# Graph attention and neighbour quantiles on one core: five record blocks in one sequence with scatters between gathers, and compare networks over two tiles at once in a planned order

## The chip, the cores and the metric

The kernel runs on one core of a Trainium2 chip. The metric is the device time of that core in microseconds (us), the median of the runs shown. One execution was taken by the hardware profiler. The engines are called PE (matrix multiply), PEld (its weight loads), DVE (vector), ACT (scalar), POOL (GpSimd, which here issues almost nothing but indirect DMAs) and SP (which issues plain DMAs).

## What is computed

There are 4,096 nodes with 128 features and an adjacency matrix of 0 and 1 in which a row holds 11 to 55 ones, 32 on average. The first layer is graph attention with 8 heads, the second replaces each node by quantiles of its neighbours:

```python
Wh = einsum('nd,hde->hne', nodes, W)
e  = leaky_relu(f1[:, :, None] + f2[:, None, :])      # f1 = Wh.a1, f2 = Wh.a2
h  = elu(softmax(where(adj > 0, e, -9e15)) @ Wh)      # 8 heads
x1 = layernorm(nodes + elu(concat(h) @ W1 + b1))
# second layer: drop every skip-th neighbour, sort the kept ones per feature
picked_q = sort(x1[kept neighbours], axis=0)[ceil(q * n_keep) - 1]   # q = .25 .5 .75
out = (0.5 * mean_q(picked_q) + 0.5 * x1) @ Wl.T + bl + x1
```

## The kernel before

Rows are worked in tiles of 128 nodes, one node to a partition, 32 tiles in all.

**First stage (attention).** `neighbours` reads the adjacency and leaves, on DVE, the list of up to 64 neighbours of each row of a tile (the search). `complete_records` finishes the records of a block of tiles, `rank_by_count` orders the block's rows by their number of neighbours, and indirect DMAs from POOL (`scatter`, L195) put the records into DRAM in that order. So the rows of one sorted tile have about equally many neighbours, and a tile needs few empty slots. There are three blocks, `BLOCKS = [4, 12, 16]` tiles, and a table `CAPS` says how many neighbours each sorted tile must hold. `layers` cuts that capacity into layers of 32, 16, 8 and 4 columns.

For one sorted tile, `list_rows` loads the records (`R`) and the narrow layers' lists with SP DMAs and transposes them on DVE. `fetch_rows` gathers neighbours from DRAM, one indirect DMA of 128 rows for each column of a layer (`gather`, L186, into the tile `G` or `Gs`). `G` has two buffers. `weigh_rows` makes the scores on DVE and ACT and multiplies on PE (`y`, L888). `transform` works on two or four finished tiles and leaves `x1` in the list `store`, from which POOL scatters it to DRAM. `step` puts this in order: the gathers of a tile, then the `x1` scatters, then the weighing of the tile before with pieces of the search between (`quota`). The order on every engine is the order in which the program is written (`manual_schedule`). At the end of a block all record scatters of the next block stand together on POOL. In the last block the records of all rows are scattered to `all_d` in the order of all 4,096 rows, for the second stage.

**Second stage (quantiles).** For each of 32 tiles POOL gathers `2 * HT[t]` neighbours' `x1` rows (22 to 62) into `vals`, of which there are five buffers and one for the largest tile (`most`). `quantile_out` runs a compare network over these slots on all 128 features at once. A stage of the network is cut into pieces of at most `TURN = 12` slots. The lower operand of a piece is first copied by ACT into a PSUM tile `low` (L1162), because DVE overwrites it; then DVE writes the minimum and the maximum (L1166). Pieces of fewer than four slots with one result are not copied. The pool `low_ps` has two buffers, and every piece takes a tile of its own:

```python
kept = lp.tile([P, TURN * D], F32, name="low")[:, 0 : k * m * D]
nc.scalar.copy(kept, low)
for end in ends:
    nc.vector.tensor_tensor(high if end else low, kept, high, ALU.max if end else ALU.min)
```

Two tiles run at a time, one stage of each in turn, the second begun when the first has eight stages left. At the end of a tile ACT scales the 3 to 14 slots that can hold a quantile (`u`, L1175), PE sums and multiplies them, and POOL scatters the result to the output.

A path for rows that exceed a capacity stands behind a flag at the end.

Of the kernel before, what the change touches and what calls it, by code (L numbers as in the profile page):

```python
# [24 lines left out]
P = 128  # L25
N = 4096
D = 128
# [19 lines left out]
CAPS = {  # L47
    4: [29, 33, 37, 63],
    12: [25, 27, 29, 30, 31, 32, 34, 35, 36, 38, 41, 63],
    16: [24, 26, 28, 29, 30, 31, 32, 32, 33, 34, 35, 36, 38, 39, 42, 63],  # L50
    32: [
        23, 24, 25, 26, 27, 27, 28, 29, 29, 30, 30, 30, 31, 31, 32, 32,
        33, 33, 34, 34, 35, 35, 36, 36, 37, 37, 38, 39, 40, 41, 44, 63,
    ],
}
BLOCKS = [4, 12, 16]

CAP = CAPS[NT]
# [4 lines left out]
HT = [(c - 1) // 2 for c in CAP]  # L63
LMAX = 2 * max(HT)
LMOST = 2 * sorted(HT)[-2]
TURN = 12
# [9 lines left out]
def layers(c):  # L76


    out = []
    s = 0  # L80
    for w in (32, 32, 16, 8, 4):
        if (c + 3) // 4 * 4 - s >= w:
            out.append((s, w))
            s += w
    return out
# [51 lines left out]
def pieces_of(g):  # L137


    b, k, stride, n = g  # L140
    if k == 1:
        parts = -(-n // TURN)
        out = []
        for i in range(parts):
            m = (n - sum(p[3] for p in out)) // (parts - i)
            out.append((b, 1, m, m))
            b += m
        return out
    if n >= TURN:
        return [p for i in range(k) for p in pieces_of((b + i * stride, 1, n, n))]  # L150
    parts = -(-k // (TURN // n))
    out = []
    for i in range(parts):
        kk = (k - sum(p[1] for p in out)) // (parts - i)
        out.append((b, kk, stride, n))
        b += kk * stride
    return out


def slots_of(tile_, g):  # L160

    b, k, stride, n = g
    if k == 1:
        return tile_[:, b : b + n, :].rearrange("p s d -> p (s d)")
    v = tile_[:, b : b + (k - 1) * stride + n, :]
    flat = v.rearrange("p s d -> p (s d)")

    return bass.AP(
        tensor=flat.tensor,
        offset=flat.offset,  # L170
        ap=[list(flat.ap[0]), [stride * D, k], [1, n * D]],
    )


def quantile_slots(t):


    ht = HT[t]
    slots = {ht - 1}
    for h in range((LOW[t] + 1) // 2 - 1, ht + 1):  # L180
        slots |= {ht - h + (h + 1) // 2 - 1, ht - h + (3 * h + 1) // 2 - 1}
    return slots

# [26 lines left out]
def kernel(  # L210
# [19 lines left out]
    recs_d = [dram.tile([n * P, REC], F32, name=f"rec{n}_d") for n in BLOCKS]  # L230
# [50 lines left out]
    for i in range(2):  # L281
        sets = {}
        for w, r in ROWS_OF.items():
            lists = const.tile([P, 32], I32, name=f"list{w}_{i}")
# [9 lines left out]
    for i, values in enumerate((LOW, CAP, HT)):  # L294
        for t, v in enumerate(values):
            if t == 0 or v != values[t - 1]:
                nc.gpsimd.memset(limits[:, i, t:], float(v))

# [18 lines left out]
    def search(t0, n):  # L317
        return neighbours(
            tc, adjp, rec, num, adj, range(t0, t0 + n), back, chunk
        )  # L320

    for _ in search(0, BLOCKS[0]):
        pass
# [15 lines left out]
    turn = [0]  # L339

    pools, uses = [attp], {}

    def step(fetch=None, pieces=None, quota=0, size=2, more=None):
        if fetch:
            weigh.append(fetch_rows(tc, pools, fetch, xt_d, uses))
        while store:
            scatter(nc, x1_d, *store.pop(0))
        if len(weigh) > 1 or (weigh and not fetch):
            R, parts = weigh.pop(0)
            place = len(members)  # L350
            members.append(R)
            turns = len(parts) + 9
            each = -(-quota // turns)
            done = 0
            for _ in weigh_rows(tc, attp, pools, pp, parts, turned, place, size, consts):
                if tails and next(tails[0], True):
                    tails.pop(0)
                for _ in range(min(each, quota - done)):
                    next(pieces, None)
                    done += 1  # L360
            quota -= done
            if len(members) == size:
                tails.append(
                    transform(tc, attp, pools[0 if size == 2 else -1], pp, more, turned.pop(0), list(members), consts, store)
                )
                members.clear()
        elif not fetch:
            while tails:
                if next(tails[0], True):
                    tails.pop(0)  # L370
        for _ in range(quota):
            next(pieces, None)

    def lists(b, i):
        turn[0] += 1
        t = sum(BLOCKS[:b]) + i
        cap = CAPS[BLOCKS[b]][i]
        return list_rows(tc, pools, narrow[turn[0] % 2], recs_d[b], i, cap, t, bad, uses)

    t0 = 0  # L380
    for b, n in enumerate(BLOCKS):
        complete_records(tc, cp, rec, num, bad, jp1, pidx, t0, n)
        ranks = rank_by_count(tc, cp, kp, num, jp1, before, oneb, t0, n)
        for i in range(n):
            scatter(nc, recs_d[b], rec[:, t0 + i, :], ranks[:, i : i + 1])
        last = b == len(BLOCKS) - 1
        if last:

            cp.release()
            adjp.release()  # L390
            wp = tc.alloc_tile_pool(name="order", bufs=1, side="right")
            cp = tc.alloc_tile_pool(name="cnt_all", bufs=2, side="right", reuse_waits="tile")
            found = rank_by_count(tc, cp, kp, num, jp1, before, oneb, 0, NT)
            ranks = wp.tile([P, NT], I32, name="ranks")
            nc.vector.tensor_copy(ranks, found)
            cp.release()
            cp = tc.alloc_tile_pool(name="lists", bufs=2, side="right", reuse_waits="tile")
            pools.append(cp)
            waiting = list(range(NT))
            sizes = [2] + [4] * ((n - 2) // 4 * 4) + [2] * n  # L400
            with tc.manual_schedule(engines=ALL):
                ready = [lists(b, 0)]
                for i in range(n):
                    if i + 1 < n:
                        ready.append(lists(b, i + 1))
                    step(ready.pop(0), size=sizes[i], more=kp)
                    for t in waiting[:4]:
                        scatter(nc, all_d, rec[:, t, 0:REC1], ranks[:, t : t + 1])
                    waiting = waiting[4:]
                    if i == n // 2:  # L410
                        R = cp.tile([P, NT, REC1], F32, name="all", bufs=1)
                        nc.sync.dma_start(R, all_d.rearrange("(t p) w -> p t w", p=P))
                        kept_rows(tc, cp, R, jp1, pidx, idx, own_i, bad, limits)
                        slot_places(tc, cp, R, picks, limits)
                for _ in range(3):
                    step(size=2, more=kp)
                count_bad(tc, cp, kp, bad, ones, total)
        else:
            pieces = search(t0 + n, BLOCKS[b + 1])
            quota = -(-BLOCKS[b + 1] * PIECES // n)  # L420
            with tc.manual_schedule(engines=ALL):
                ready = [lists(b, 0)]
                for i in range(n):
                    if i + 1 < n:
                        ready.append(lists(b, i + 1))
                    step(ready.pop(0), pieces, quota, more=kp)
                for _ in pieces:
                    pass
        t0 += n
# [8 lines left out]
    order = sorted(range(NT), key=lambda t: HT[t])  # L438
    order = order[0::2] + order[1::2][::-1]
    with tc.tile_pool(name="late", bufs=1) as late, tc.tile_pool(name="sort", bufs=5) as sp, tc.tile_pool(  # L440
        name="fin", bufs=3
    ) as fp, tc.tile_pool(name="low_ps", bufs=2, space=PSUM) as lp, tc.tile_pool(
# [4 lines left out]
        waiting = list(order)  # L447
        lists, running, outs = [], [], []

        def fetch_list():  # L450
            t = waiting.pop(0)
            n = 2 * HT[t]
            if n > LMOST:
                vals = sp.tile([P, LMAX, D], F32, name="most", bufs=1)
            else:
                vals = sp.tile([P, LMOST, D], F32, name="vals")
            for j in range(n):
                gather(nc, vals[:, j, :], x1_d, idx[:, t, j : j + 1])
            xs = fp.tile([P, D], F32, name="xs", bufs=6)
            gather(nc, xs, x1_d, own_i[:, t : t + 1])  # L460
            lists.append((t, vals, xs))

        def begin():
            t = lists[0][0]
            stages = len(selection_network(2 * HT[t], quantile_slots(t)))
            work = quantile_out(
# [949 lines left out]
```

## Time and profile before

| | us |
|---|---|
| median of 3 runs (3865.35 to 3875.0) | 3873.15 |
| profiled execution, its own time | 3874.47 |
| its span, first to last instruction | 3872.7 |
| POOL: first gather of the first stage | 122.6 |
| POOL: last gather of the first stage begins | 2000.3 |
| POOL: first gather of the second stage | 2047.2 |
| DVE: first compare of the second stage | 2076.3 |
| POOL: last output scatter begins | 3867.3 |

In the profile a row names the source line, the engine, the operation, what it writes and reads, the shape of both, and how often it ran. The busy time, the mean of one, the idle time of the engine just before these instructions and what ended it follow. An arrow `<-` behind an idle time names the releaser.

### The profile page before, as it was taken

The page shows a single profiled execution, that of the slowest core. Times are in us where ns is not written, and L with a number is a line of the kernel's source. Part 1 is how long each engine was busy: PE and PEld are TensorE (multiplying, and loading weights), DVE is VectorE, ACT ScalarE, POOL GpSimd, SP SyncE. Part 2 cuts the span into 40 slices and gives each one's busy share as a digit, 9 for nine tenths or more (in the row PEclk, how much of TensorE's full clock was granted, in tenths as well). Part 3 has the DMA queues.
Part 4 walks back from the last instruction along what each step waited for, and adds up shares of the span by engine and source line. Part 5 has one row for each costly group of instructions (what it writes and reads, how often), then busy time and mean ns, then how long its engine had stood idle before and what let it go on. Part 6 is the DMA issues. An engine that isn't in the chain of part 4 may idle for free. (4 is left out here: it accounts for less than half of the span.)

```text
span 3872.7 us, 17731 instructions
## 1 busy us (share of the span) xinstructions
PE 747.5 (19%) x2799; PEld 466.1 (12%) x2801; DVE 2613.9 (67%) x4953; ACT 1204.0 (31%) x1902; POOL 2320.1 (60%) x2452
## 2 busy tenths in 40 slices
PE   2023143334303231334330110000000010000001
PEld 1011022112202211111220100000000000000001
DVE  6798366657702111522214899999999999999987
ACT  3132123324102122221222433434444444344343
POOL 0676177777736677777756777777763345455520
PEclk9966566557656665666665555555555555555555
DMA  5542234334212122222211111111110011111100
GB/s 182 145 154 76 86 97 128 108 99 118 50 38 49 47 49 49 63 55 57 56 43 46 52 52 52 52 52 52 52 47 25 24 27 39 29 36 40 42 17 3
DMA packets 114202, 241.10 MB, mean 62 GB/s; under 512 B 50880, under 2 KB 67264, under 8 KB 105888
## 3 DMA queue, kind: packets, MB, share of 16 engines
q0 software_dynamic: 76224, 161.01, 16.5%
q10 hardware_dynamic: 12160, 68.49, 5.1%
q1 hardware_dynamic: 25696, 10.38, 1.3%
q14 instruction: 96, 0.79, 0.1%
q8 instruction: 26, 0.43, 0.0%
HBM read 228.53 MB, written 11.18 MB: 62 GB/s over the span
## 5 line engine op out<-in xcount | busy, mean ns | idle before, releaser
L1166 DVE TENSOR_TENSOR vals<-low,vals 128x1024 f32<-128x1024 f32 (+9 forms) x1359 | 1403.0, 1058 | 178.8 <-ACT low L1162 106.1
L186 POOL DMA_INDIRECT G<-xt_d,idx x1096 | 1099.1, 1003 | 470.0 <-issue 325.6
L186 POOL DMA_INDIRECT vals<-x_d,idx x960 | 911.6, 950 | 294.9 <-issue 283.4
L1162 ACT COPY low<-vals 128x1024 f32<-128x1024 f32 (+10 forms) x701 | 607.0, 876 | 983.5 <-DVE vals L1166 925.9
L888 PE MATMUL y<-G,pf 128*64 128x258 f32 (+1 forms) x1184 | 249.3, 492 | 837.6 <-DVE pf L866 765.1
L1176 PE MATMUL st_ps<-ident,u 128*128 128x128 f32 x344 | 83.3, 427 | 1662.5 <-ACT u L1175 1559.5
L195 POOL DMA_INDIRECT out_dram<-o,own_i x32 | 31.8, 993 | 467.2 <-ACT o L1188 462.0
L852 DVE TENSOR_TENSOR z<-G,f1x 128x256 f32<-128x256 f32 (+3 forms) x44 | 21.9, 498 | 418.7 <-DMA G<-xt_d,idx 411.2
L1176 PEld LDWEIGHTS st_ps<-ident,u 128*128 128x128 f32 x344 | 73.8, 320 | 1671.3 <-ACT u L1175 1567.9
L901 ACT COPY raw<-y 32x258 f32<-32x258 f32 (+1 forms) x472 | 172.2, 365 | 315.2 <-PE y L888 219.1
L854 ACT ACTIVATE z<-z 128x256 f32<-128x256 f32 (+3 forms) x60 | 20.0, 334 | 804.1 <-DVE z L853 804.1
L888 PEld LDWEIGHTS y<-G,pf 128*64 128x64 f32 (+1 forms) x1184 | 134.8, 183 | 940.9 <-DVE pf L866 753.1
L589 DVE MAX8 first<-sgn 128x8 f32<-128x128 bf16 x1024 | 209.5, 276 | 1.9
L561 ACT ACTIVATE sgn<-adj_t 128x2048 bf16<-128x2048 int32 x64 | 122.0, 1906 | 152.6 <-DVE first L589 118.0
L792 DVE TENSOR_SCALAR bad<-R 128x1 f32<-128x1 f32 x32 | 4.6, 145 | 209.9 <-DMA R<-rec_d 209.9
L1166 DVE TENSOR_TENSOR most<-low,most 128x1024 f32<-128x1024 f32 (+7 forms) x116 | 131.9, 1167 | 2.6 <-ACT low L1162 0.7
L195 POOL DMA_INDIRECT rec_d<-rec,ranks x32 | 30.9, 967 | 156.1 <-DVE ranks L732 100.1
L949 PE MATMUL o<-hv,W_sb 128*128 128x256 f32 (+1 forms) x208 | 85.9, 537 | 196.2 <-DVE hv L943 196.2
L1166 DVE TENSOR_TENSOR vals<-vals 128x256 f32<-128x256 f32 (+2 forms) x335 | 119.0, 410 | 0.0
L908 DVE TENSOR_SCALAR rden<-raw 128x8 f32<-128x8 f32 x32 | 6.7, 208 | 163.2 <-ACT raw L901 163.2
L601 DVE MAX8 rec<-first 128x8 f32<-128x256 f32 x256 | 108.7, 425 | 6.6
L921 ACT COPY yT<-turned 128x512 f32<-128x512 f32 x64 | 65.3, 1020 | 153.6 <-PE turned L920 147.7
(180 smaller groups left out, 1841.2 us busy)
## 6 DMA issues: line engine op xcount, KB each, us to landing
adj_t<-in_adj_dram ACTq DMA_DIRECT2D x64, 1024.0 KB
G<-xt_d,idx POOLq DMA_INDIRECT x1096
vals<-x_d,idx POOLq DMA_INDIRECT x960
R<-rec_d SPq DMA_DIRECT2D x128, 26.4 KB
xt_d<-rec SPq DMA_DIRECT2D x4, 548.0 KB
rec<-in_x_dram SPq DMA_DIRECT2D x4, 512.0 KB
score<-rec_d SPq DMA_DIRECT2D x120, 1.0 KB
Gs<-xt_d,idx POOLq DMA_INDIRECT x88
```

What stands on the lines that cost most here:

```text
L186: nc.gpsimd.indirect_dma_start(out=dst, out_offset=None, in_=rows, in_offset=bass.IndirectOffsetOnAxis(ap=idx, axis=0),)
L195: return nc.gpsimd.indirect_dma_start(out=rows, out_offset=bass.IndirectOffsetOnAxis(ap=idx, axis=0), in_=src, in_offset=None,)
L561: nc.scalar.activation(sgn, adj_t, AF.Sign, accum_out=cnt[:, i : i + 1])
L589: nc.vector.max(first[:, ts(c0 // CW + c, 8)], key[:, b * (512 // CW) + c, :])
L601: nc.vector.max(top, first)
L888: nc.tensor.matmul(yv[p0 : p0 + m], lhsT=pf[:, c : c + m], rhs=rhs, start=(i == 0), stop=(i == len(parts) - 1), skip_group_check=True,)
L901: nc.scalar.copy(raw[p0 : p0 + m, 4 * half + b - 1 : 4 * half + b + 1, :], y[p0 : p0 + m, :, a : a + D + 1],)
L921: nc.scalar.copy(yT[:, :, ts(place, P)].rearrange("p h (u g) -> p g u h", u=4)[:, ts(half, 16)], t_ps.rearrange("p b (g u h) -> p (b g) u ...
L949: nc.tensor.matmul(o, lhsT=consts["W1_sb"][:, h, :], rhs=hv[:, ts(j, n)], start=(h == 0), stop=(h == H - 1),)
L1162: nc.scalar.copy(kept, low)
L1166: nc.vector.tensor_tensor(high if end else low, kept, high, ALU.max if end else ALU.min)
L1176: nc.tensor.matmul(st_ps, lhsT=u, rhs=ident, start=(i == 0), stop=(i == len(terms) - 1))
```

## The change

1. `BLOCKS` becomes `[4, 6, 8, 8, 6]`. All 32 tiles are one sequence: records are loaded two tiles ahead (`load`, SP), prepared one tile ahead (`prep`, DVE), and the search of the next block is spread over all tiles of a block but the last.
2. `fetch_rows` calls `between` after every third gather, which issues one waiting scatter. `x1`, record and `all_d` scatters all go this way.
3. `LAYERS` replaces `CAPS` and `layers`: a layer `(s0, w, g0)` starts at column `g0`, so that only some row groups of a tile get it.
4. In the second stage most tiles are worked in pairs of equal size (`UNITS`); a piece may take the same slots of both tiles. `TURN` becomes 14. `vals` has three buffers for up to 80 slots.
5. `plan_units` fixes at build time, with costs written into it, the order of loads, pieces, sums and outputs. It takes two units at a time and the piece that it reckons ready first.
6. The lower operands go into the two halves of one tile, `low[:, turn % 2, :]`, 14 slots each.

The list `EARLY` is empty, so the code for a first stage on POOL is never issued.

```diff
-BLOCKS = [4, 12, 16]
-TURN = 12
+BLOCKS = [4, 6, 8, 8, 6]
+UNITS = [(0,), (1,), (30,), (31,)] + [(t, t + 1) for t in range(28, 3, -2)] + [(2,), (3,)]
+TURN = 14
+EARLY = []
...
+COPY, COMPARE, FETCH, LAND = (150, 107), (110, 133), 1250, 2200
+def plan_units(buffers):
...
+        if copied:
+            ring = [ring[1], clock["dve"] + 50]
...
+            weigh.append(fetch_rows(tc, pools, ready.pop(k), xt_d, uses, put_one))
+            while aside:
+                put_one()
+            if end and b < final:
+                load(k + 1)
+                load(k + 2)
+            work(k - 1, behind, left, soon)
+            if end and b < final:
+                prep(k + 1)
...
-    with tc.tile_pool(name="late", bufs=1) as late, tc.tile_pool(name="sort", bufs=5) as sp, tc.tile_pool(
-        name="fin", bufs=3
-    ) as fp, tc.tile_pool(name="low_ps", bufs=2, space=PSUM) as lp, tc.tile_pool(
+    with tc.tile_pool(name="late", bufs=1) as late, tc.tile_pool(name="sort", bufs=3) as sp, tc.tile_pool(
+        name="fin", bufs=2
+    ) as fp, tc.tile_pool(name="low_ps", bufs=1, space=PSUM) as lp, tc.tile_pool(
...
+        plans, events = plan_units(3)
+        work, outs, turn = {}, [], 0
+        low = lp.tile([P, 2, TURN * D], F32, name="low")
+        for kind, u, *rest in events:
...
+            elif kind == "piece":
+                compare(nc, low[:, turn % 2, :], work[u][0], n, *rest)
+                turn += rest[-1]
...
+        for g in range(g0, w):
+            gather(nc, G[:, col + g - g0, :], xt_d, idx[:, g : g + 1])
+            done += 1
+            if done % 3 == 0:
+                between()
...
+def compare(nc, room, vals, n, who, g, d, ends, copied):
+    b, k, stride, m = g
+    low, high = slots_of(vals, n, who, g), slots_of(vals, n, who, (b + d, k, stride, m))
+    kept = low
+    if copied:
+        kept = room[:, 0 : len(who) * k * m * D]
...
+        nc.scalar.copy(kept, low)
+    for end in ends:
+        nc.vector.tensor_tensor(high if end else low, kept, high, ALU.max if end else ALU.min)
```

## Prediction

> **What bounds the kernel now.** I read the page first, then the groups with shapes kept apart, the waits of each stage, and the timeline of the end. The page's tenths (97 us a digit) show two stages.
>
> ```profile
> PE 747.5 (19%) x2799; PEld 466.1 (12%) x2801; DVE 2613.9 (67%) x4953; ACT 1204.0 (31%) x1902; POOL 2320.1 (60%) x2452
> ...
> DVE  6798366657702111522214899999999999999987
> ACT  3132123324102122221222433434444444344343
> POOL 0676177777736677777756777777763345455520
> ```
>
> In the first stage (digits 2 to 21) POOL is full but for its issue gaps and DVE is not: POOL bounds it, from the first gather at 122.6 to the second stage's first at 2047.2, 1,924.6 us. In the second stage DVE stands at 9 throughout while POOL falls to half: DVE bounds it.
>
> ```profile
> L186 POOL DMA_INDIRECT G<-xt_d,idx x1096 | 1099.1, 1003 | 470.0 <-issue 325.6 <-PE y L888 70.4 <-DVE sgn L582 61.8
> L1166 DVE TENSOR_TENSOR vals<-low,vals 128x1024 f32<-128x1024 f32 x542 | 653.3, 1221 | 53.7 <-ACT low L1162 33.2 <-DMA vals<-x_d,idx 9.8
> L1162 ACT COPY low<-vals 128x1024 f32<-128x1024 f32 x271 | 273.0, 1015 | 361.8 <-DVE vals L1166 346.5 <-DMA vals<-x_d,idx 8.0 <-DVE most L1166 7.0
> L1166 DVE TENSOR_TENSOR vals<-low,vals 128x1536 f32<-128x1536 f32 x138 | 242.3, 1756 | 38.1 <-ACT low L1162 35.3
> L1162 ACT COPY low<-vals 128x1536 f32<-128x1536 f32 x69 | 99.4, 1441 | 99.9 <-DVE vals L1166 96.7 <-DMA vals<-x_d,idx 3.2
> ```
>
> From these: a compare of 8 slots takes 1.221 us, of 12 slots 1.756, so 0.134 us a slot and 0.15 fixed; a copy takes 1.015 and 1.441, so 0.107 a slot and 0.16 fixed. The copies are 672 us of ACT in all. What they cost DVE now is in the waits of the second stage:
>
> ```profile
> ACT low L1162 <- DVE vals L1166: 954.1, 532, 19.8
> ...
> DVE vals L1166 <- ACT low L1162: 106.1, 135, 4.5
> DVE vals L1166 <- DMA vals<-x_d,idx: 45.8, 2, 36.0
> ```
>
> ACT waits for DVE, hardly the other way: 566 us of copying are hidden beside compares, because a copy has its own `low` buffer and runs one piece ahead. At the very end, where only one tile is left and its data forbid that, the price of a copy with no cover is seen:
>
> ```profile
> 3839.86 1.23 ACT L1162 COPY low<-vals 128x1280 f32<-128x1280 f32 x1 [2.10 <-DVE vals L1166]
> 3841.12 3.02 DVE L1166 TENSOR_TENSOR vals<-low,vals 128x1280 f32<-128x1280 f32 x2 [1.29 <-ACT low L1162]
> 3844.17 0.59 ACT L1162 COPY low<-vals 128x512 f32<-128x512 f32 x1 [3.08 <-DVE vals L1166]
> 3844.79 1.42 DVE L1166 TENSOR_TENSOR vals<-low,vals 128x512 f32<-128x512 f32 x2 [0.66 <-ACT low L1162]
> ```
>
> DVE stands 1.29 us for a copy of 1.23, 0.66 for one of 0.59: the whole copy and 0.033 us for each of two handovers.
>
> **The change, first stage.** *Gathers:* the layers sum to 1,152 columns where they were 1,184. A gather costs 1.298 us of POOL (busy 1,185.5 and issue 351.2 over 1,184): -42 us. *Scatters:* those that now follow each other wait for the one before to land. The waits of POOL in this stage are 52.1 for `rec_d`, 36.9 for `all_d`, 25.7 for `x1_d`, 115 us together. With three gathers (3.9 us) between two scatters that wait is over; the four record scatters of the first block and the last six of `x1` stay together, about 15 us: -100. *Waits for G:* these are 70.4 + 61.8 (the latter also ends as PE's last `y` of the tile before ends, at 473.4; POOL goes on at 473.2). A block's last tile fills both buffers of `G`, so the next block's first gather waits until that tile is weighed. That boundary now comes four times instead of twice. Its price: in the 16th tile PE's last `y` ended 11 us after the last score `z`, in tiles with search pieces between (5, 7, 9, 11) 20 to 27. So 2 us of landing and 25, 25, 20 and 11: about 89. The record loads no longer stand in it, since the record scatters end at about half of the last tile's gathers. The first block has 25 search pieces a tile (before: 36), which leaves about 15 us of `G` waits and 10 for rank; a scatter of `x1` now stands behind three gathers of its tile instead of all, and if DVE is late, gathers queue behind it: 5. Sum 119 against 132: -13. *End:* 44 small DVE operations for row capacities and two more table loads come before the first `vals` gather: +8. *Hidden:* 128 more SP DMAs at 0.42 us, two tiles ahead of use, and 14 more parts at about 1.7 us of DVE; DVE is busy 897 of 1,940 us here. If POOL were not the bound, the parts would cost 25. Sum -147: the second stage starts at 1,900.
>
> **The change, second stage.** *Compares:* running the network functions gives 1,823 compares over 10,766 slots before (1,715 us by the rows) and 1,383 over 10,881 after. Pairs make larger pieces; that is 1,664 us, -51. Pieces of 14 slots have no row: 80 at 2.02 by the slope, at most two of 7 slots (2.18), +13. Pieces over two tiles have one more dimension than any seen: between nothing and 5% (80 us); I take nothing, since strided and flat pieces share a row here and the 12-slot form reaches 1.759 at most with a mean of 1.756.
>
> *Copies:* 714 instead of 761, 722 us. Here the diff does not tell enough. In the built program's order the two halves of `low` are one tile, and a copy waits for the last compare that read either half. The same is so when the units differ:
>
> ```
> DVE compare vals_9960  <- low[second half]   waits ACT 1218, then DVE = 3711
> ACT copy    low[first half] <- vals_10262    waits DVE >= 3711, then ACT = 1219
> DVE compare vals_10262 <- low[first half]    waits ACT 1219
> ```
>
> Nothing of the second line needs the first. I counted for each copy what stands on DVE between the compare that it waits for and the one that reads it: nothing for 649 of 714, less than the copy for 33, enough for 14, no such wait for 18. With each copy's row and two handovers the uncovered time is 727 us. The same count on the program of before gives 88; its trace has 106.1. So the count is trusted to some 20 us. ACT copies, then DVE compares, then ACT copies.
>
> *Sums:* 179 scalings (172 before), 0.32 us each (1.28 for four at the end of the timeline), stand on ACT after a unit's last compare and before the next copy: 57 us that DVE now waits. *Start:* 22 gathers before the first compare, as before, 29 us. Units 0 and 1 then occupy DVE to +125 and the third is gathered by +111, so no gap. *Gathers:* six more, 8 us; POOL needs about 1,370 of the stage and is ahead, so hidden. Were DVE faster, a pair (80 gathers, 100 us) would still load within the 127 to 207 us of the unit ahead. *Tail:* 7 us as before (3861.4 to 3868.2).
>
> 29 + 1,664 - 10 (compares that still overlap; 83 before) + 727 + 57 + 7 = 2,474, against 1,821 before.
>
> *A rule against the reading.* No row has one PSUM tile shared by two engines. The Trainium skill, "PSUM — Partial Sum Buffer", section "PSUM bank collisions raise a hardware error", says that two engines must be kept apart by bank and quadrant of partitions. A bank holds 512 fp32, so 14 slots are 3.5 banks: the halves share the fourth bank, and only a first-half piece of 13 or more slots would need a guard. There are 40 copies of 14 slots, about 20 in that half, each with a neighbour on both sides: 40 copies x 1.7 = 68 us instead of 727, and a total of about 3,710. But ACT obeys the semaphores that the program has, not those that would do. I take 727.
>
> **Sum.** Span 3,872.7 - 147 + 653 = 4,379; the profiled execution's own time is 1.8 above its span and 1.3 above the median: 4,379.
>
> **The rivals.** *The copies do overlap* (slower turns to faster): the order was planned for a ring of two halves, and if a copy ran while DVE compares from the other half, DVE would wait some 60 us. 29 + 1,664 - 60 + 60 + 30 + 7 = 1,730, total 3,872.7 - 147 - 91 = 3,635. It decides below 220 us of uncovered copies, under a third of them. For it: the planned order. Against: the wait counts, and that they foretell the old trace. *The first stage gains nothing:* four boundaries with search pieces in DVE's queue cost 27 to 60 each (61.8 is on record), and scatters wait for late `x1`. Then 4,525. *Two-tile pieces are slower:* +80, 4,460. *Partly covered:* uncopied pieces and scalings hide 100 to 300 us more than counted, 4,080 to 4,280. *The change does not act:* a row above its partial layers' capacity would start the general path; with this adjacency none is above, and it would cost far more than any case here.
>
> **How the numbers follow.** As summed 0.72 (4,300 to 4,460 by the first stage +-50 and the copies +-50), no gain in the first stage 0.12, slower pieces 0.06, partly covered 0.06: all slower. Overlap 0.04, faster. Same, within 0.3% or 12 us, which is about what a measurement of this kernel can tell from no change, needs two errors that cancel: 0.01 of the partly covered. Range 4,285 to 4,500: it leaves out overlap, most of partly covered and part of no gain.
>
> **What would show it.** Right: DVE's second-stage wait for `low` near 730 us in some 680 waits of about a copy's length; DVE tenths of 6 or 7 there; POOL half idle; the first `vals` gather near 1,900; four POOL waits for `y` of 13 to 30 us; no waits of `rec_d` for `rec_d` past the first block. Wrong: a wait for `low` below 300 us, a first `vals` gather after 2,000, or mean compares off the 1.221 and 1.756 rows.

## The result, and the profile after

| | us |
|---|---|
| median before (4 runs, 3865.35 to 3879.51) | 3874.07 |
| median after (4 runs, 4390.35 to 4393.87) | 4392.65 |
| ratio, 95 % interval | 1.134 (1.1319 to 1.1362) |
| span of the profiled execution after | 4390.7 |
| first gather of the second stage, before / after | 2047.2 / 1878.3 |
| second stage, from there to the end of the span | 1825.5 / 2512.4 |

The change makes the kernel 13 % slower. The first stage became 169 us shorter, the second 687 us longer. The page of the kernel after, first its busy times, then the same tenths as were shown of the kernel before (110 us a digit now):

```profile
PE 768.3 (17%) x2874; PEld 484.0 (11%) x2877; DVE 2684.1 (61%) x4706; ACT 1268.7 (29%) x1866; POOL 2290.3 (52%) x2450
...
DVE  7766845673455321656666666666666666666666
ACT  3222322322222111322223233332332333332333
POOL 0675775776777677567755050604415532354220
```

From the 18th digit on DVE, which stood at 9 in the kernel before, stands at 5 and then 6, and POOL has holes down to 0. No engine is full, so something is handed back and forth between engines. The waits of the kernel after say what:

```profile
ACT low L1440 <- DVE vals L1442: 1660.5, 690, 4.2
POOL vals L342 <- ACT u L703: 1001.4, 13, 133.7
DVE vals L1442 <- ACT low L1440: 778.7, 684, 4.5
```

Each line gives the waiting engine and tile, the releaser, the time in total, how often, and the longest. ACT waits 690 times for DVE, and DVE 684 times for ACT, with 714 copies in all. 1,660.5 is about the time for which DVE is busy in this stage (1660.1), and 778.7 about that of the copies (722.9), the handovers and the scalings. Each engine waits for as long as the other works: they take turns. POOL's 1,001 us follow from this: it waits for buffers of `vals` that are held longer (1,008 us in e8 and 287 in e6 below, which differ in `low` alone). The timeline of the kernel after, in the middle of the stage (start, duration, what ran, and in brackets the idle time before it; the rows of POOL are left out):

```profile
3000.02 3.55 DVE L1442 TENSOR_TENSOR vals<-low,vals 128x1536 f32<-128x1536 f32 x2 [1.51 <-ACT low L1440]
3003.60 1.44 ACT L1440 COPY low<-vals 128x1536 f32<-128x1536 f32 x1 [3.62 <-DVE vals L1442]
3005.08 3.55 DVE L1442 TENSOR_TENSOR vals<-low,vals 128x1536 f32<-128x1536 f32 x2 [1.51 <-ACT low L1440]
3008.66 1.02 ACT L1440 COPY low<-vals 128x1024 f32<-128x1024 f32 x1 [3.62 <-DVE vals L1442]
3009.71 2.48 DVE L1442 TENSOR_TENSOR vals<-low,vals 128x1024 f32<-128x1024 f32 x2 [1.08 <-ACT low L1440]
```

Compares end at 3003.57, the copy starts at 3003.60, ends at 3005.04, and the next compares start at 3005.08. For the kernel before, the prediction showed such a row of copies without cover at the very end; in all, its DVE waited 106.1 us for `low`.

The first four runs below (e1 to e4) were made on another chip, on which the kernel before takes 4330.29 us (23 runs, 4299.79 to 4343.37, at granted clocks of 0.577 to 0.589, where the profile before has 0.587), so each ratio is to the kernel before on the run's own chip.

### The profile page after: what moved, and what is told of

Its sections match the earlier page's. It is cut to its first block, busy times and chain, and to the rows that moved or that the text cites. A ratio compares the mean times of both kernels' runs of the same rounds, so it can differ in the third digit from the quotient of the medians.

```text
span 4390.7 us, 17374 instructions
## 1 busy us (share of the span) xinstructions
PE 768.3 (17%) x2874; PEld 484.0 (11%) x2877; DVE 2684.1 (61%) x4706; ACT 1268.7 (29%) x1866; POOL 2290.3 (52%) x2450
## 5 line engine op out<-in xcount | busy, mean ns | idle before, releaser
L1442 DVE TENSOR_TENSOR vals<-low,vals 128x1024 f32<-128x1024 f32 (+9 forms) x1292 | 1629.2, 1261 | 841.6 <-ACT low L1440 778.7
L342 POOL DMA_INDIRECT vals<-x_d,idx x1028 | 971.4, 945 | 1315.2 <-ACT u L703 1001.4
L1440 ACT COPY low<-vals 128x1024 f32<-128x1024 f32 (+8 forms) x714 | 722.9, 1012 | 1714.5 <-DVE vals L1442 1660.5
L704 PE MATMUL fin<-ident,u 128*128 128x128 f32 x358 | 81.2, 418 | 2044.4 <-ACT u L703 1966.4
L1167 PE MATMUL y<-G,pf 128*64 128x258 f32 (+1 forms) x1232 | 277.1, 497 | 654.9 <-DVE pf L1139 550.9
L704 PEld LDWEIGHTS fin<-ident,u 128*128 128x128 f32 x358 | 75.5, 321 | 2051.3 <-ACT u L703 1972.6
L1239 PE MATMUL key<-yT,W_sb 128*128 128x256 f32 (+1 forms) x240 | 102.5, 582 | 16.6 <-ACT yT L1200 16.6
L1199 PE MATMUL turned<-ident,raw 128*128 128x128 f32 x256 | 65.7, 406 | 153.6 <-DVE raw L1190 79.5
L856 DVE MATCH_REPLACE8 first<-rec,first 128x256 f32<-128x256 f32 x224 | 91.4, 408 | 0.0
L1139 DVE TENSOR_TENSOR pf<-z,own 128x512 f32<-128x512 f32 (+2 forms) x134 | 79.7, 635 | 8.0 <-PE y L1167 7.8
```

Of the source, the lines that this page charges most:

```text
L342: nc.gpsimd.indirect_dma_start(out=dst, out_offset=None, in_=rows, in_offset=bass.IndirectOffsetOnAxis(ap=idx, axis=0),)
L704: nc.tensor.matmul(fin[:, i, :], lhsT=g, rhs=ident, start=(a == 0), stop=(a == len(terms) - 1), skip_group_check=True,)
L856: nc.vector.match_replace(first, top, first, 0.0)
L1167: nc.tensor.matmul(yv[p0 : p0 + m], lhsT=pf, rhs=rhs, start=not any(over[:i]), stop=not any(over[i + 1 :]), skip_group_check=True,)
L1239: nc.tensor.matmul(hT[:, ts(j, n)], lhsT=consts["W_sb"][:, h, :], rhs=yT[:, h, 0:n], start=True, stop=True,)
```

## The experiments

**Theory:** the shared tile `low` makes copies and compares take turns, and this alone makes the second stage long. **Rivals:** the planned order or the two-tile pieces are slow in themselves; pieces of 14 slots, whose halves end within a bank of PSUM by the page that the prediction cites, get in each other's way; and, for the first stage, that its gain is not the gathers and scatters.

**e1 and e2: one half of the change at a time.** e1 has the first stage of before and the second of after; e2 the first of after and the second of before.

```diff
 # e2, in the kernel after (its edit in short)
-UNITS = ...; TURN = 14; plan_units; compare(nc, low[:, turn % 2, :], ...)
+TURN = 12; quantile_out as in the kernel before
```

> The first stage of before with the second stage of the change. If the uncovered copies are the loss, the second stage is as long as in the changed kernel (2,508 us where before has 1,821), so 4,560, with a DVE wait for low near 779. If the loss is an interplay with the new first stage (memory handed over later, lists in another order), it stays near 3,874 or anywhere below 4,500.

> The first stage of the change with the second stage of before. If the two stages add up, the second stage starts near 1,878 instead of 2,047 and the rest is as before: 3,705. If the new first stage costs something that only shows later, it is above 3,750.

e1: 4887.12 us, ratio 1.1296 (1.126 to 1.1331). e2: 4329.46, ratio 1.0003 (0.999 to 1.0017). The whole loss comes with the second stage: from the first gather of `vals` to the end it is 1,990 us with the old networks (e2) and 2,545 with the new (e1). The absolute times expected were missed, for on this chip both stages with old code are longer: the old first stage takes 2335.8 us to the first gather of `vals` (2047.2 in the table above), the old networks 1,990 (1,825.5). DVE's wait for `low` in e1 was 587.1 in 519 waits, not 779; another 215.3 us before the same compares are put down to "issue", which means that the profile shows no releaser. And e2's gain of 169 us in the first stage did not come: gathers of `vals` begin at 2343.0 in e2 and at 2335.8 in e1. POOL's waits in e2 (`x_d` is the profile's name for the tensor of `x1`):

```profile
POOL G L209 <- PE y L997: 303.7, 13, 43.9
POOL x_d L218 <- DVE x L1116: 89.6, 8, 44.9
```

In the kernel after the first of these was 88.1 in 4 waits. So on this chip POOL does not set the pace of the first stage, but waits for the engines that use its gathers. What makes them late there was not found. Against e5, which is the same kernel on the faster chip, instructions last about as long (compares 1,058 and 1,057 ns on the average), but ACT, before it copies `y`, stands 537.5 us in 36 waits whose releaser the profile calls "remote", and e5 has no such wait. So this chip loses time not in longer instructions but in waits that the trace doesn't explain. e5 asks the same again on a chip where the kernel before takes its recorded time.

**e3 and e4: a buffer for each copy.** e3 takes for every copied piece a PSUM tile of its own, of two (12 slots a piece, since two tiles of 14 were not tried in PSUM). e4 keeps the one tile with its halves and 14 slots, and puts it into SBUF.

```diff
 # e3
-TURN = 14
+TURN = 12
-        low = lp.tile([P, 2, TURN * D], F32, name="low")
-                compare(nc, low[:, turn % 2, :], work[u][0], n, *rest)
-                turn += rest[-1]
+                if rest[-1]:
+                    low = lp.tile([P, TURN * D], F32, name="low", bufs=2)
+                compare(nc, low, work[u][0], n, *rest)
 # e4
-        low = lp.tile([P, 2, TURN * D], F32, name="low")
+        low = late.tile([P, 2, TURN * D], F32, name="low")
```

> The changed kernel with a PSUM tile of its own for every copied piece, two buffers, and TURN = 12 so that both and the sums fit. If the one shared tile is the cause, DVE's wait for low falls from 779 to below 100 and the time to 3,590 to 3,700, faster than before. If pairs, three buffers or the planned order are the cause, the wait turns into one for gathers and it stays above 4,100.

> The changed kernel with the same one tile of two halves of 14 slots, but in SBUF. In its program a copy waits only for the compare two pieces back. If the wait is what counts, the time falls to 3,590 to 3,700 with the tile still shared. If it is PSUM or its banks that make copies and compares take turns, the same; if two SBUF operands cost DVE or POOL more, compares rise above 1.221 and 1.756 us or gathers above 0.945, and it is slower than the kernel with two PSUM tiles. If pairs or the plan are the cause it stays above 4,100.

e3: 4209.7 us, ratio 0.9719 (0.9687 to 0.9751). e4: 4239.63, ratio 0.9798 (0.9767 to 0.9829). Against e1's second stage of 2,545 us, e3's is 1,872 and e4's 1,898. DVE's wait for `low` falls to 97.1 (e3) and 55.5 (e4), with 73.3 and 13.8 more that the profile puts to "issue" or "remote". The same networks in the same planned order are faster than the old ones (1,990 in e2) once each copy has a buffer that is free. e4 says what the program's waits go by: two halves of one SBUF tile count as two, two halves of one PSUM tile as one.

**e5 and e6: the same on a chip like that of the first table.** e5 is e2's kernel, e6 is e3's.

> The kernel before with the first stage of the change and the old quantile networks. Theory (the new first stage gives what the two recorded profiles show, 2047.2 - 1878.3 = 169 us, wherever the gathers of POOL set its pace): first gather into vals at about 1,880, ratio to the kernel before 0.956 (169 of 3,870 saved). Rival (as the run e2_first_only had it: the first stage is paced by something other than POOL's gathers, and the order of scatters and partial layers is worth nothing): first gather into vals no earlier than in the kernel before, ratio 1.000. Which holds is read from POOL's wait for G behind the PE together with the start of the second stage.

> The changed kernel with a PSUM tile of its own for every copied piece (two buffers, 12 slots instead of 14). Theory (the shared tile makes copies and compares take turns): the second stage falls from 2,508 to about 1,866 as in e3_two_tiles, the wait of the compares for low from 779 to about 97; with a first stage of 1,878 the time is about 3,750 (ratio 0.967), with a first stage as long as that of the kernel before 0.972 again. Rival (the e3 gain was tied to how the first stage ended there): ratio nearer to 1.0, the wait for low back above 300.

e5: 3709.06 us, ratio 0.9586 (0.957 to 0.9602); first gather of `vals` at 1876.6. e6: 3634.68, ratio 0.9389 (0.9373 to 0.9404); there it is 1878.0. Here the first stage gives what the two profiles showed. The second stage lasts 1,830.5 us in e5, 1,755.3 in e6 and 2,512.4 in the kernel after. The page and the waits of e6:

```profile
DVE  7685685467734555321537999999999999999997
...
ACT low L1441 <- DVE vals L1443: 909.9, 619, 19.7
...
POOL vals L342 <- ACT u L704: 287.1, 12, 50.2
...
DVE vals L1443 <- ACT low L1441: 74.5, 48, 4.5
DVE vals L1443 <- DMA vals<-x_d,idx: 36.1, 2, 30.0
```

DVE is back at 9, ACT waits for DVE and hardly the other way. In the timeline of e6 twelve compares follow each other without a gap, and copies run beside them:

```profile
2699.19 17.50 DVE L1443 TENSOR_TENSOR vals<-low,vals 128x1024 f32<-128x1024 f32 x12
...
2700.45 1.44 ACT L1441 COPY low<-vals 128x1536 f32<-128x1536 f32 x1 [1.37 <-DVE vals L1443]
...
2702.84 1.02 ACT L1441 COPY low<-vals 128x1024 f32<-128x1024 f32 x1 [0.95 <-DVE vals L1443]
```

e6 beats both kernels, by 6 % and by 17 %. It came out lower than the 3,750 expected, because that sum took 1,866 us for the second stage, from e3, and the stage is longer on e3's chip.

**e7: the shared buffer put into the kernel before.** One number is changed.

```diff
-tc.tile_pool(name="low_ps", bufs=2, space=PSUM)
+tc.tile_pool(name="low_ps", bufs=1, space=PSUM)
```

> The kernel before with one buffer instead of two for its low tile, and nothing else changed: its networks, one tile at a time, stay. Theory (one PSUM tile for all copies is enough to lose the time): the copies that no compare covers go from 88 to 626 us, so the second stage is longer by some 540 us and the kernel by a ratio of about 1.14; the compares' wait for low is over 550 in nearly every copy. Rival (the loss belongs to networks of two tiles in the planned order, and before has slack that a single buffer only uses up): under 150 us, ratio below 1.04.

4452.0 us, ratio 1.1499 (1.148 to 1.1518). The waits of e7:

```profile
ACT low L1162 <- DVE vals L1166: 1441.8, 669, 7.4
...
DVE vals L1166 <- ACT low L1162: 576.6, 626, 5.6
...
DVE most L1166 <- ACT low L1162: 55.5, 56, 1.5
```

With old networks, old order and pieces of one tile, a loss of the same kind and nearly the same size comes, 581 us where 540 were expected: 576.6 + 55.5 = 632 us of waiting, where the count on the program had given 626. Neither the plan nor the two-tile pieces are needed for it.

**e8: 12 slots, halves kept.** The control for e6, which differs from the kernel after in two things. By the page that the prediction cites, halves of 12 slots are three whole banks, so they don't end within one.

```diff
-TURN = 14
+TURN = 12
```

> The changed kernel with pieces of at most 12 slots instead of 14, its two halves of one PSUM tile kept: the control for the run with a tile for every piece, which has 12 too. Theory (the size of a piece is worth nothing, the shared tile all): uncovered copies 733 instead of 727 us, a wait for low of about 785, time within 0.5% of the changed kernel, ratio to the kernel before about 1.13. Rival (halves of 14 slots lie across the banks of PSUM[...] and that makes copy and compare get in each other's way): the wait falls to near 97, ratio about 0.97.

4407.3 us, ratio 1.1384 (1.1365 to 1.1403), 0.3 % above the kernel after. The waits of e8:

```profile
ACT low L1440 <- DVE vals L1442: 1671.6, 713, 3.9
...
DVE vals L1442 <- ACT low L1440: 790.5, 712, 4.5
```

Between e8 and e6 the tile is the only difference: 790.5 us against 74.5. Whether the halves end within a bank or not makes no difference to it.

**e9: scatters in a row.** e6 without change 2, so that the scatters of a tile go out behind its gathers.

```diff
             done += 1
-            if done % 3 == 0:
-                between()
```

> The changed kernel with a PSUM tile for every copied piece (as e6_two_tiles) but without the scatters between the gathers: each tile's scatters go out one after another behind its gathers, as in the kernel before. Theory (of the 169 us that the new first stage gives, the spread of the scatters gives about 100): the waits of scatters for the scatter ahead of them come back at some 100 us (52.1 + 36.9 + 25.7 = 114.7 before, about 12 in the changed kernel), the first gather into vals moves from 1,878 to about 1,980, and the time from 3,635 to about 3,735 (ratio to the kernel before 0.965). Rival (POOL has to wait for the PE to set G free at those places in any case, so that the scatters' waits only take the place of the waits for G): first gather into vals under 1,900, time within 20 us of e6_two_tiles, ratio below 0.945, with the waits for G smaller by what the scatters wait more.

3818.0 us, ratio 0.9854 (0.9838 to 0.9871). The first gather of `vals` is at 2057.7, 180 us later than in e6; the theory had said 100, the rival nothing. The second stage is unchanged (1,756). POOL's waits in the first stage of e9:

```profile
POOL G L342 <- PE y L1166: 150.2, 4, 53.9
...
POOL rec_d L351 <- DMA rec_d<-rec,ranks: 53.1, 27, 4.9
POOL all_d L351 <- DMA all_d<-rec,order: 45.4, 28, 2.4
POOL G L342 <- DVE first L857: 36.6, 1, 36.6
...
POOL x_d L351 <- DMA x_d<-x,R: 17.8, 10, 4.0
```

The three waits of a scatter for the one ahead make 116 us, as expected. But the waits for `G` make 150.2 + 36.6 where e6 has 89.8. DVE's wait for a tile's records, in the first stage of e9 and then of e6, says why:

```profile
DVE bad L1057 <- DMA R<-rec_d: 228.1, 6, 60.3
```

```profile
DVE bad L1057 <- DMA R<-rec_d: 53.2, 5, 16.5
```

When a block's record scatters are the last thing before its first tile, its records are loaded late, DVE can prepare that tile only then, and the gathers of the next stand behind it. With five blocks this comes four times, so five blocks without spread scatters end their first stage later (2057.7) than three blocks did (2047.2). In this kernel five blocks pay only with the spread. (Of the two waits, 105 us of scatters for scatters and 97 for `G` more than in e6, 22 don't show in the end: POOL's own work and issue in that stage are shorter in e9, its busy time by 12 us.) What the blocks and the new layers give by themselves was not run.

## Why the prediction was right, step by step

It said 4,379; 4392.65 was measured. The mechanism was the one that was foreseen. That the total came within 14 us is in part luck, for the first stage came out 22 us shorter than said and the second some 35 longer.

*Uncovered copies (727) and scalings (57): right.* Sum 784, DVE's wait for `low` 778.7, in 684 waits where some 680 were named. The count of uncovered copies on the program stood on record before the run for the kernel after, e7 and e8; for e6 it did not, where 97 was expected from e3. Scalings come on top where a unit's sums stand right behind its last compare. In e7 they don't: there the other tile's compares run meanwhile (the scalings of 2538.41, for one, beside compares that start at 2538.51).

| kernel | counted, us | waited for `low`, us |
|---|---|---|
| before | 88 | 106.1 |
| after | 727 + 57 | 778.7 |
| e6, a tile for each copy | 16 + 57 | 74.5 |
| e7, before with one tile | 626 | 632.1 |
| e8, shared, 12 slots | 733 + 57 | 790.5 |

*The rule on PSUM: rightly not taken.* By the Trainium skill, "PSUM — Partial Sum Buffer", section "PSUM bank collisions raise a hardware error", two engines need a guard where they meet in a bank and quadrant, which made 68 us and a total of about 3,710 (its terms sum to 3,720). In e8 the halves are 1,536 columns, three whole banks by the page's 512, so by that rule no guard is called for (provided that the tile starts at the border of a bank, which no run here shows), and 790.5 us are lost all the same: the waits are those that the program carries.

*Compares and two-tile pieces: right.* 1,664 was said for the compares, DVE was busy 1660.1. The piece of 14 slots, which had no row, and the 12-slot piece of the kernel after:

```profile
L1442 DVE TENSOR_TENSOR vals<-low,vals 128x1536 f32<-128x1536 f32 x274 | 481.6, 1758 | 214.2 <-ACT low L1440 203.4 <-DMA vals<-x_d,idx 4.5 <-DMA out_dram<-o,own_i 1.5
L1442 DVE TENSOR_TENSOR vals<-low,vals 128x1792 f32<-128x1792 f32 x80 | 161.9, 2024 | 70.2 <-ACT low L1440 65.4 <-DMA vals<-x_d,idx 3.4
```

2.024 where 2.02 was worked out, and 1.758 with two tiles among them where 1.756 was the old row. A copy of 14 slots took 1.656. So the rival of slower pieces is out: they cost nothing.

*Second stage as a whole: 34 us short.* 2,474 was said for what took 2,508.5 to the end of the last output scatter, and 2,512.4 to the end of the span. DVE's waits for gathered rows of `vals` were 40.6 in 8, not the 29 of the start alone: 12. Of the 10 us said to overlap some 6 are not there (1660.1 busy against 1,664 - 10). The other half, some 20 us, is idle time of DVE in this stage for which its list of waits has no line.

*First stage: 22 us better than said.* The second stage began at 1878.3 instead of 1,900. Gathers (-42) follow from the count. The scatters' waits for each other fell to 8.0 for `rec_d` and 6.2 for `x_d`; 15 was said for what stays. The 20.4 for `lanef` below stands where the kernel before waited 24.1 at its end. The four boundaries cost 88.1 where 89 was said:

```profile
POOL G L342 <- PE y L1167: 88.1, 4, 26.9
...
POOL x_d L351 <- DVE lanef L638: 20.4, 1, 20.4
...
POOL x_d L351 <- DVE x L1286: 10.0, 1, 10.0
```

The term that was mis-sized is the 30 us for the first block's `G` waits, rank and late `x1`: only the 10.0 us for `x` came, and no `G` wait for PE beyond the four. e9 adds that the terms are not independent. Taking away the spread alone cost 180 us, more than the whole gain of 169. The prediction says that record loads "no longer stand" in the boundary between blocks, because the scatters end earlier; that sentence is worth some 97 us (186.8 against 89.8 of waits for `G`), which the sum had not priced.

*The rival that copies overlap* was worked out at 3,635. e6, where they do, took 3634.68: a second stage of 1,755 (1,730 said) after a first of 1,878 (1,900). That 3,635 is met so closely is luck: the first stage is 22 us shorter than in that sum and the second 25 longer, and e6 has 12 slots a piece instead of 14. But the plan does what it was made for once its two halves are two tiles.

## What to carry to other kernels

When two engines pass a buffer back and forth, read the wait in both directions: if both are long, and each nearly as long as the other's busy time, they take turns, and the number of buffers that the program really sees is one. A ring made of slices of one tile is a ring only if the program's waits go by slices; look at the waits of the built program before trusting a plan that counts two. And spread scatters between gathers where what they write is loaded soon after: here the waits of scatters for scatters were only about half of what it saved (105 us beside 97).

## What else the runs show of the hardware

With `low` in SBUF (e4) instead of PSUM (e3, same chip) the gathers themselves took POOL longer, which the expectation of e4 had named as possible. The groups of e3 and then of e4:

```profile
L342 POOL DMA_INDIRECT vals<-x_d,idx x1028 | 990.7, 964 | 698.4 <-ACT u L704 382.2 <-issue 305.7 <-DMA vals<-x_d,idx 5.2
```

```profile
L342 POOL DMA_INDIRECT vals<-x_d,idx x1028 | 1332.8, 1297 | 374.6 <-issue 307.2 <-ACT u L703 58.3 <-DVE total L1344 4.8
```

1,297 ns a gather instead of 964, for the same 1,028 gathers (963 in e1, which has 14 slots as e4 has, but in PSUM), and DVE's wait for `vals` is 178.5 us in e4 against 37.9 in e3. The compares hardly change (1,224 and 1,755 ns for 8 and 12 slots in e4). The Trainium skill, "SBUF — State Buffer", section "SBUF: two separate sides", says that a DVE instruction with two SBUF inputs holds a pair of ports shared with GpSimd, against GpSimd work that reads SBUF; the only operand that moved here is `low`, from PSUM to SBUF, and it is POOL that became slower. The timeline of e4 agrees that it is the compares: gathers that start beside them, from 2880.67 to 2900.53, take 0.94 to 2.09 us, and from 2903.76 to 2923.72, where DVE stands, each takes 0.94. That the ports are the mechanism was not tested by itself.

Compares of pieces that follow each other directly also overlap a little, as the prediction had it with its 10 us instead of 83. In e6 the group of compares with copies has 1,342 with a mean of 1,215 ns, which makes 1,630 us, and was busy for 1581.0; in the kernel after 1,292 with 1,261 ns make 1,629 us, and it was busy for 1629.2. In the same way DVE is busy for 1,689 us in the second stage of e7, and for 1,640 with the same compares in the kernel before. So taking turns loses some 50 us of overlap beside the waits.
